# Ten buffers in turn for the pieces of x, four of them in the weights' space, each load issued behind a store

## The chip, the cores and the metric

The kernel runs on one core of a Trainium2 chip. The metric is the device time of one execution in microseconds (us). The times before are three executions of the same program; one more execution was taken by the hardware profiler, and all rows of "the profile" come from that one. Engine names are those of the profile: PE (TensorE, matrix products), DVE (VectorE), ACT (ScalarE), POOL (GpSimd), SP (SyncE, which here only issues transfers).

## The reference

One layer of a relational graph network on 12500 nodes with 256 features and 212500 edges, in float32. Its core, with eight relations (`edge_type` from 0 to 7) and edges sorted by `dst`:

```python
h  = maximum(layernorm(x), 0)
hx = einsum('ni,rio->rno', h, weight)            # 8 matrices of 256 x 256
agg = segment_sum(hx[edge_type, src], dst)       # sum over the edges of a node
out = x + agg * sqrt(0.5) + bias + (h @ loop_weight) * sqrt(0.5)
```

## The kernel before

**Order of the sums.** The kernel does not form `hx`. It first sums, for each node and each relation, the rows of h of its sources, and multiplies by the eight matrices afterwards. The edges are cut into 1581 tiles of up to 128. For each tile, 128 rows of 1 KB are fetched by their index into a message buffer (`msg`, `gather`, lines 922 to 946); this is an indirect transfer that POOL issues, one for each tile, save for 50 tiles whose rows SP and ACT fetch one by one. DVE makes a one-hot matrix for four tiles (`onehots`, L993), PE multiplies it with the message rows (`edge_sums`, L1031), and DVE adds the result of two tiles to an accumulator in a ring (`add_sums`, L1064). When a group of 128 nodes is complete, PE multiplies its accumulators with the eight matrices `w` and its own row of h with `wl` (`product`, L1238), and the result with x and the bias is stored.

**The start.** The rows of h, that is the normalised x, must be in memory before messages can be fetched from them. x is cut into 26 pieces (24 of 512 rows, 512 KB each; one of 128 rows; one of 84). A piece is loaded into a row buffer (`load_rows`, L886, on SP), DVE takes its statistics (`bn_stats`, L828), ACT takes the root (L864) and normalises it in place (L872, four instructions in a piece), and SP stores it to `h32` (`rest`, L895). `norm_rows(i)` does this for piece i; what it leaves for later runs in the `after` functions that `close` returns. Pieces 0 to 3 are done ahead of the main loop. In the loop over tiles t, three of four turns take one piece each, so that the last piece is taken at t = 28.

**Tiles from x.** The gathers begin before h32 exists. Tiles 0 to 99 are fetched from x itself, and their messages are normalised by DVE and ACT in the message buffer (`batch`, L1402, and `moments_by_scalar` for a share of the statistics on ACT). From tile 100 on gathers read h32 (`state["h32"]` = 28 + AHEAD, then LATE more); the first of them waits for all the stores.

**What sets the order.** All instructions are placed by hand (`tc.manual_schedule()`): each engine runs its instructions in the order in which this code issues them, and waits in that order. Four orders matter here.

- SP's queue carries the loads and stores of the pieces, the index loads (L390, L406, L418), then bias and weights (`load_weights`, L1363, issued at t = 28 behind the last store), then the rows of x and h of the node groups (`load_groups`, L1181). A load into a buffer waits on SP until the store of the buffer's last piece has landed. Before, `norm_rows(i)` first issues the load of piece i + 4, which takes the buffer of piece i - 2 among six; the store of piece i comes later, in `after`.
- POOL's gathers are issued ahead of the sums by `goal(t)` (L948): at most 24 + 2t early on, t + 65 later, with less lead from t = 170 on. Each gather also waits for the sums of the last pair of tiles issued before it (L945), and for its message buffer, one of 66 (33 pairs).
- ACT normalises pieces, then messages; at t = 34 it scales the weights (`scale_weights`, L1378), in place, in the order w (first half), wl, w (second half), wl.
- PE turns the rows of the first node group (L1088) soon after; these rows (`hr`) come from h32 by SP, behind the weights.

**The space of w.** `w` holds 128 partitions of 2 x 2048 floats, 16 KB in each partition, from the start of the kernel; a piece of x takes 4 KB in each partition. `rowp` has six row buffers (`ROWS`), which the pieces, the bias and later the rows of the node groups take in turn.

Of the kernel before, what the change touches and what calls it, by code (L numbers as in the profile page):

```python
# [9 lines left out]
F32 = mybir.dt.float32  # L10
# [13 lines left out]
P = 128  # L24
# [4 lines left out]
XG = 4  # L29
# [56 lines left out]
SHARED = 3  # L86

ROWS = 6
FIRST = 4


# [157 lines left out]
def kernel(  # L249
# [12 lines left out]
    N, D = x.shape  # L262
# [30 lines left out]
    w = const.tile([P, KC, R * D], F32, name="w")  # L293
# [34 lines left out]
    with ExitStack() as main:  # L328
# [4 lines left out]
        ep = main.enter_context(tc.tile_pool(name="ep", bufs=1))  # L333
        rowp = main.enter_context(tc.tile_pool(name="rowp", bufs=ROWS))
        idx = main.enter_context(tc.tile_pool(name="idx", bufs=2))
# [469 lines left out]
        for d in range(0, N, XG * P):  # L805
            k = min(XG, (N - d) // P)
# [4 lines left out]
        def rows_of(a, i):  # L811
            d, k, n = pieces[i]
            return a[d : d + k * n].rearrange("(k p) d -> p k d", p=n)
# [3 lines left out]
        def moments(rows_, n, then, begun=None):  # L817

            if not bunch:
                bunch.append(small.tile([P, 2 * BATCH, 6], F32, name="stats") if begun is None else begun)  # L820
                if n < P:
                    nc.vector.memset(bunch[0], 0.0)
            stats = bunch[0]
            here = rows_ if begun is None else rows_[:-SHARED]
            for row in rows_:
                k = sum(len(r) for r, _, _ in bunch[1:])
                if begun is None or len(bunch) - 1 < len(here):
                    in_run("stats", nc.vector.bn_stats(stats[:n, k, :], row), row is here[-1])  # L828
                bunch.append(([row], n, None))
            bunch.append(([], n, then))  # L830
# [49 lines left out]
        xts = {}  # L880

        def load_rows(i):
            if i < len(pieces):
                _, k, n = pieces[i]
                xts[i] = rowp.tile([P, XG, D], F32, tag="rows", name="xt")
                nc.sync.dma_start(xts[i][:n, :k, :], rows_of(x, i))  # L886

        def norm_rows(i):
            d, k, n = pieces[i]
            xt = xts.pop(i)  # L890
            if i > 1:
                load_rows(i + ROWS - 2)

            def rest():
                nc.sync.dma_start(rows_of(h32, i), xt[:n, :k, :])  # L895

            moments([xt[:n, j, :] for j in range(k)], n, rest)

# [103 lines left out]
        def load_offsets(u0):  # L1002
            n = min(REGS, NU - u0)
            b, q = row_of(u0)
            _, vals = nc.values_load_multi_w_load_instructions(
                place[b][0:1, q : q + n], engines=[DVE], min_val=0, max_val=RING - 1,
                skip_runtime_bounds_check_because="clamped to the ring where it is computed")
            for i, v in enumerate(vals):
                offsets[u0 + i] = v
# [279 lines left out]
        with tc.manual_schedule():  # L1289

            load = prepare(0)
            load[0]()
            for i in range(ROWS):
                load_rows(i)
            make_identity(nc, ident)
            iota_i = marks.tile([P, XG * GROUP], I32, tag="mark0", name="iota_i")
# [29 lines left out]
            for i in range(2):  # L1326
                norm_rows(i)
# [19 lines left out]
            after.pop(0)()  # L1347
            for i in range(2, FIRST):
                norm_rows(i)
# [83 lines left out]
            load_offsets(0)  # L1433
            done["norm"] = FIRST
            for t in range(0, 2 * BATCH, BATCH):
# [5 lines left out]
            for t in range(NT):  # L1441
# [12 lines left out]
                if t % BATCH == BATCH - 1:  # L1454
                    if done["norm"] < len(pieces):
                        after = batch(t + 1 + BATCH)
                    elif done["scaled"] <= t + 1 + 2 * BATCH:
                        after = batch(done["scaled"], 2 * BATCH)
                        after.append(lambda t=done["scaled"]: begin_batch(t))
                elif done["norm"] < len(pieces):  # L1460
                    for i in range(1 if NT > 400 else 20):
                        if done["norm"] < len(pieces):
                            norm_rows(done["norm"])
                            done["norm"] += 1
                            if t % BATCH % 2 or NT <= 400 or done["norm"] == len(pieces):
                                after += close()
                    if NT <= 400:
                        for f in after:
                            f()
                        after = []  # L1470
                    if done["norm"] == len(pieces):
                        for f in after:
                            f()
                        after = []
                        norms_end(t)
# [91 lines left out]
```

## Time and profile before

| what | value |
|---|---|
| median of three executions | 1952.6 us |
| lowest and highest | 1951.16 and 1956.97 us |
| the profiled execution | 1951.46 us |
| its span, first to last instruction | 1949.8 us |
| granted TensorE clock in it, mean | 0.953 of full speed |
| bytes moved by DMA in it | 279.41 MB |

How to read the rows. A row of a timeline gives start and length in us, engine, line, operation, output and inputs, how many instructions are merged in it (x8), and in brackets the idle time of the engine before it with what ended that idle time. A row of waits gives the engine and line that waited, what for, the total in us, how often, and the longest. A row of stretches gives the limits in us, the length, for each engine its busy time with the number of instructions (PE, PEld for weight loads, DVE, ACT, POOL), the granted clock, the mean busy share of the 16 DMA engines, and GB/s; a share over 1 arises where transfers overlap. Busy time does not hold waiting or the time to issue a transfer.

### The profile page before, as it was taken

How to read it: one execution, taken by the hardware profiler on the slowest of the kernel's cores; microseconds unless marked ns; L12 is line 12 of the kernel's file. 1: busy time of each engine (PE TensorE's matmuls, PEld its weight loads, DVE VectorE, ACT ScalarE, POOL GpSimd, SP SyncE). 2: the span in 40 equal slices, each digit the busy share in tenths (PEclk: the TensorE clock that was granted, in tenths of full speed). 3: DMA queues.
4: the chain of work that ended last, by engine and by line, in shares of the span. 5: the costliest groups of instructions: out<-in, count | busy, mean ns of one | idle time of the engine just before them, and what ended most of it. 6: DMA issues, size and time to landing. Idle time of an engine off the chain costs nothing.

```text
span 1949.8 us, 40539 instructions
## 1 busy us (share of the span) xinstructions
PE 1702.0 (87%) x10161; PEld 1460.0 (75%) x10161; DVE 1305.0 (67%) x3284; ACT 157.2 (8%) x333; POOL 1455.6 (75%) x1557
## 2 busy tenths in 40 slices
PE   2358999999998999889898899998889889899998
PEld 2247898998887777777777777777777777687887
DVE  7668766787765687656677665578566567665652
ACT  6778200000000000000000000000000000000000
POOL 7767777777777777777777777777777777777774
PEclk9559999999999999999999999999999999999999
DMA  9984454544444444444544444444444444444442
GB/s 291 329 281 129 125 152 123 153 133 141 122 142 131 132 143 114 138 131 121 152 132 121 141 128 124 142 121 142 131 120 140 130 125 132 121 141 126 131 121 82
DMA packets 158423, 279.41 MB, mean 143 GB/s; under 512 B 35441, under 2 KB 109191, under 8 KB 158183
## 3 DMA queue, kind: packets, MB, share of 16 engines
q0 software_dynamic: 73488, 200.77, 35.6%
q1 hardware_dynamic: 76648, 72.73, 12.1%
q10 hardware_dynamic: 8046, 3.30, 0.9%
q8 instruction: 80, 1.31, 0.3%
q14 instruction: 161, 1.31, 0.2%
HBM read 251.06 MB, written 25.60 MB: 142 GB/s over the span
## 4 chain that ended last, share of the span: by engine, by line
PE 40%; DMA 23%; POOL 20%; issue 8%; DVE 6%; ACT 3%; SPq 0%; DVEq 0%; POOLq 0%; ACTq 0%; PEldq 0%
PE po L1238 20%; DMA msg<-h,gidx 20%; POOL msg L936 20%; PE ps L1031 18%; ACT msg L872 1%; DVE acc L1064 1%; DMA h<-xt 1%; DVE stats L828 1%; DMA xt<-in_x_dram 1%; DVE acc L1106 1%; PE pt L1088 1%; ACT xt L872 1%; DMA msg<-h 1%; DVE oh L993 1%; PE pt L1137 1%
## 5 line engine op out<-in xcount | busy, mean ns | idle before, releaser
L936 POOL DMA_INDIRECT msg<-h,gidx x1431 | 1358.7, 949 | 437.4 <-issue 363.8
L1031 PEld LDWEIGHTS ps<-oh,msg 128*128 128x128 f32 x6324 | 929.1, 197 | 390.5 <-DMA msg<-h,gidx 248.4
L1031 PE MATMUL ps<-oh,msg 128*128 128x136 f32 (+1 forms) x6324 | 1010.5, 289 | 204.5 <-DMA msg<-h,gidx 120.8
L1238 PE MATMUL po<-w,acc 128*128 128x256 f32 (+1 forms) x3136 | 890.3, 389 | 7.8 <-DVE acc L1064 7.2
L1064 DVE TENSOR_TENSOR acc<-acc,ps 128x352 f32 x791 | 408.6, 517 | 391.2 <-PE ps L1031 381.9
L1238 PEld LDWEIGHTS po<-w,acc 128*128 128x128 f32 (+1 forms) x3136 | 519.4, 193 | 45.5 <-DVE acc L1064 10.4
L1106 DVE SCALAR_TENSOR_TENSOR acc<-types,pt 128x256 f32<-128x256 bf16 x688 | 248.6, 412 | 68.6 <-PE pt L1088 64.4
L993 DVE TENSOR_TENSOR oh<-fixed,cols 128x544 f32<-128x544 f32 x396 | 282.8, 714 | 0.0
L936 POOL DMA_INDIRECT msg<-in_x_dram,gidx x100 | 94.9, 949 | 39.2 <-issue 34.2
L1238 PE MATMUL po<-wl,self_t 128*128 128x256 f32 (+1 forms) x392 | 114.6, 418 | 6.8 <-DVE acc L1064 4.5
L1238 PEld LDWEIGHTS po<-wl,self_t 128*128 128x128 f32 (+1 forms) x392 | 72.9, 208 | 15.5 <-DVE acc L1064 5.6
L1226 DVE TENSOR_TENSOR xr<-xr,po 128x256 f32<-128x256 f32 (+1 forms) x98 | 40.5, 413 | 24.0 <-PE po L1238 17.3
L872 ACT ACTIVATE msg<-msg,shift,rstd 128x256 f32<-128x256 f32 x100 | 50.8, 587 | 6.3 <-DVE stats L836 4.6
L872 ACT ACTIVATE xt<-xt,shift,rstd 128x256 f32<-128x256 f32 x98 | 50.0, 587 | 13.1 <-DVE shift L869 13.1
L1253 DVE TENSOR_TENSOR xr<-xr,po 128x256 f32<-128x256 f32 (+1 forms) x98 | 41.2, 421 | 10.6 <-PE po L1238 7.3
L828 DVE BATCH_NORM_STATS2 stats<-xt 128x6 f32<-128x256 f32 x98 | 34.1, 411 | 14.9 <-DMA xt<-in_x_dram 14.6
L1088 PE MATMUL pt<-ident,hr 128*128 128x128 f32 (+1 forms) x196 | 39.0, 282 | 4.6 <-DMA hr<-h 2.7
L1093 DVE COPY self_t<-pt 128x256 f32<-128x256 f32 (+1 forms) x98 | 40.5, 414 | 3.1 <-PE pt L1088 2.9
L1160 DVE CAST types<-pt 128x512 bf16<-128x512 f32 x22 | 15.2, 691 | 40.5 <-PE pt L1156 40.5
L455 DVE TENSOR_SCALAR moves<-fixed 128x271 int32<-128x271 int32 (+1 forms) x90 | 40.5, 450 | 1.6 <-DVE acc L1064 0.5
L457 DVE COPY_PREDICATED fixed<-moves,fixed 128x311 int32<-128x311 int32 (+14 forms) x90 | 38.0, 422 | 3.1
L1088 PEld LDWEIGHTS pt<-ident,hr 128*128 128x128 f32 (+1 forms) x196 | 25.7, 152 | 7.1 <-DMA hr<-h 2.9
(166 smaller groups left out, 348.8 us busy)
## 6 DMA issues: line engine op xcount, KB each, us to landing
msg<-h ACTq DMA_DIRECT2D x3200, 1.0 KB
msg<-h SPq DMA_DIRECT2D x3200, 1.0 KB
msg<-h,gidx POOLq DMA_INDIRECT x1431, 4.7
xt<-in_x_dram SPq DMA_DIRECT2D x24, 512.0 KB
h<-xt SPq DMA_DIRECT2D x24, 512.0 KB
xr<-in_x_dram SPq DMA_DIRECT2D x23, 512.0 KB
hr<-h SPq DMA_DIRECT2D x23, 512.0 KB
out_dram<-xr SPq DMA_DIRECT2D x22, 512.0 KB
```

The lines of the kernel that those rows point to most:

```text
L455: nc.vector.tensor_single_scalar(m, packed[:, :n], 1 << (bit + k), op=ALU.bitwise_and)
L828: in_run("stats", nc.vector.bn_stats(stats[:n, k, :], row), row is here[-1])
L872: nc.scalar.activation(row, row, AF.Relu, bias=shift[:n, j : j + 1], scale=rstd[:n, j : j + 1])
L936: i = nc.gpsimd.indirect_dma_start(out=msg[t], out_offset=None, in_=table[:, :], in_offset=bass.IndirectOffsetOnAxis(ap=gidx[b][:, at : at ...
L993: j = nc.vector.tensor_tensor(o[:, k : k + v, :i, :width], iota_f[:, :width].unsqueeze(1).unsqueeze(1).to_broadcast([P, v, i, width]), of. ...
L1031: j = nc.tensor.matmul(ps[:, c, first : first + width], m[:, c * P : (c + 1) * P], o[:, :width], start=(i == 0 and c == 0), stop=(end and ...
L1064: i = nc.vector.tensor_tensor(a, a, ps, op=ALU.add)
L1088: in_run("turns", nc.tensor.transpose(pst[:, c, :n], rows_[:n, c * P : (c + 1) * P], ident[:n, :n]), c == KC - 1)
L1093: nc.vector.tensor_copy(got["self", g][:, :, :n], pst[:, :, :n])
L1106: i = nc.vector.scalar_tensor_tensor(acc[:, :, r, s0 : s0 + n], of, float(r + 1), pst[:, :, :n], op0=ALU.is_equal, op1=ALU.mult)
L1238: i = nc.tensor.matmul(got["out", g][:n], lhs, rhs, start=(r == R and c == 0), stop=(r == R - 1 and c == KC - 1))
L1253: nc.vector.tensor_add(rows_[:n, k, :], rows_[:n, k, :], got["out", g][:n])
```

## The change

The number of places for pieces of x goes from six to ten (`STAGED`). Piece i takes place i mod 10; places 0 to 5 are row buffers as before, places 6 to 9 are quarters of the space of `w`, which the weights fill later. Ten loads are issued at the start instead of six. From then on the load of piece i + 8 is issued right behind the store of piece i, in `rest`, where before the load of piece i + 4 was issued at the start of `norm_rows(i)`, ahead of that store. Both wait for the store of piece i - 2, whose place they take. The pieces that take the quarters of `w` are 6 to 9 and 16 to 19. Of 26 pieces, 18 take a row buffer, three for each of the six, so the tiles that follow in `rowp` begin at the first buffer.

```diff
 ROWS = 6
+STAGED = 10
 FIRST = 4
...
         def load_rows(i):
             if i < len(pieces):
                 _, k, n = pieces[i]
-                xts[i] = rowp.tile([P, XG, D], F32, tag="rows", name="xt")
+                j = i % STAGED - ROWS
+                if j < 0:
+                    xts[i] = rowp.tile([P, XG, D], F32, tag="rows", name="xt")
+                else:
+                    xts[i] = w.rearrange("p c (a k d) -> p (c a) k d", k=XG, d=D)[:, j, :, :]
                 nc.sync.dma_start(xts[i][:n, :k, :], rows_of(x, i))
 
         def norm_rows(i):
             d, k, n = pieces[i]
             xt = xts.pop(i)
-            if i > 1:
-                load_rows(i + ROWS - 2)
-
             def rest():
                 nc.sync.dma_start(rows_of(h32, i), xt[:n, :k, :])
+                if i > 1:
+                    load_rows(i + STAGED - 2)
 
             moments([xt[:n, j, :] for j in range(k)], n, rest)
...
             load = prepare(0)
             load[0]()
-            for i in range(ROWS):
+            for i in range(STAGED):
                 load_rows(i)
             make_identity(nc, ident)
```

## The prediction, made before the result was known

> **What bounds the kernel now.** I read the page first, then the gathers on POOL as a timeline, then stretches of the span.
>
> ```profile
> span 1949.8 us, 40539 instructions
> PE 1702.0 (87%) x10161; PEld 1460.0 (75%) x10161; DVE 1305.0 (67%) x3284; ACT 157.2 (8%) x333; POOL 1455.6 (75%) x1557
> ```
>
> PE looks like the bound at 87%, POOL like a bystander at 75%. But POOL's share leaves out the issue gap of about 0.30 us after each gather. The stretch from 205.7 us to the last gather counts them:
>
> ```profile
> 205.70:1933.00 1727.30, 1588.52 (x9610) 1361.73 (x9609) 1149.80 (x2746) 6.92 (x4) 1307.21 (x1377) 0.98 0.46 132
> ```
>
> 1377 gathers in 1727.3 us are 1.254 us each, which is 0.949 busy plus 0.305 of gap: POOL runs without a stop from 205.7 us on, and the other engines follow its data. The timeline of POOL (start, length, idle before in brackets) holds every stop:
>
> ```profile
> 4.86 1.11 POOL L936 DMA_INDIRECT msg<-in_x_dram,gidx  x1 [2.23 <-DVE bound_o L1320]
> ...
> 94.01 0.95 POOL L936 DMA_INDIRECT msg<-in_x_dram,gidx  x1 [0.30 <-issue]
> 100.54 0.94 POOL L936 DMA_INDIRECT msg<-in_x_dram,gidx  x1 [5.59 <-issue]
> ...
> 109.29 0.95 POOL L936 DMA_INDIRECT msg<-in_x_dram,gidx  x1 [0.30 <-issue]
> 112.07 0.94 POOL L936 DMA_INDIRECT msg<-in_x_dram,gidx  x1 [1.83 <-issue]
> ...
> 137.06 0.95 POOL L936 DMA_INDIRECT msg<-h,gidx  x1 [0.30 <-ACT wl L1379]
> ...
> 203.69 0.95 POOL L936 DMA_INDIRECT msg<-h,gidx  x1 [0.30 <-issue]
> 205.66 0.95 POOL L936 DMA_INDIRECT msg<-h,gidx  x1 [1.01 <-ACT msg L872]
> ...
> 1931.94 0.95 POOL L936 DMA_INDIRECT msg<-h,gidx  x1 [0.30 <-issue]
> ```
>
> Three stops beyond 0.30 us: 5.29, 1.53 and 0.71, together **7.53 us**. Removing them is all that an earlier start phase can give; what follows is POOL's own pace and a fixed tail of 17.9 us (1949.8 less 1931.94).
>
> What are they waits for? Counting POOL's rows, the gather at 100.54 is that of tile 72, emitted in turn 26 and tied by L945 to the sums of tile 25; that at 112.07 is tile 80, tied to tile 29; that at 205.66 is tile 154, tied to tile 89, whose message buffer it reuses. PE's timeline answers to it (tile 25 ends early in the first row, tile 29 in the second, tile 89 is the last row):
>
> ```profile
> 99.02 2.09 PE L1031 MATMUL ps<-oh,msg 128*128 128x104 f32 x8 [5.72 <-DVE acc L1064]
> 110.55 2.09 PE L1031 MATMUL ps<-oh,msg 128*128 128x104 f32 x8 [2.13 <-DVE acc L1064]
> 137.98 0.54 PE L1088 MATMUL pt<-ident,hr 84*128 84x84 f32 x2 [2.70 <-DMA hr<-h]
> 203.89 0.99 PE L1031 MATMUL ps<-oh,msg 128*128 128x104 f32 x4
> ```
>
> So two gates: the pieces being normalised up to turn 29, and the tiles normalised on ACT and DVE (28 to 99) up to tile 89. **First gate.** The waits of SP and DVE, then ACT's timeline:
>
> ```profile
> SPq L886 <- DMA h<-xt: 57.6, 18, 6.4
> DVE stats L828 <- DMA xt<-in_x_dram: 14.6, 6, 3.1
> ```
>
> ```profile
> 69.95 0.30 ACT L864 ACTIVATE rstd<-spread,eps 128x8 f32<-128x8 f32 x1 [1.57 <-DVE spread L862]
> 83.45 0.30 ACT L864 ACTIVATE rstd<-spread,eps 128x8 f32<-128x8 f32 x1 [3.85 <-DVE spread L862]
> 98.58 0.30 ACT L864 ACTIVATE rstd<-spread,eps 128x8 f32<-128x8 f32 x1 [5.52 <-DVE spread L862]
> 110.11 0.30 ACT L864 ACTIVATE rstd<-spread,eps 128x8 f32<-128x8 f32 x1 [1.93 <-DVE spread L862]
> 131.43 1.91 ACT L1378 ACTIVATE w<-w 128x2048 f32<-128x2048 f32 x1
> 134.79 1.91 ACT L1378 ACTIVATE w<-w 128x2048 f32<-128x2048 f32 x1 [1.15 <-DMA w<-in_L_gnn_weight_dram]
> ```
>
> SP stands 57.6 us in 18 waits for a store before it may refill the buffer. The late pieces then cost DVE 14.6 us, and ACT's four idle times sum to 12.87 us (10.94 by turn 25). **Second gate.** The second half of w lands only at 134.8 us, and ACT, in order, normalises no tile past it meanwhile; hr, behind w on SP, stops PE at 137.98.
>
> **The change part by part.** The transfers that it moves, from the list of DMA issues:
>
> ```profile
> xt<-in_x_dram SPq DMA_DIRECT2D x24, 512.0 KB
> h<-xt SPq DMA_DIRECT2D x24, 512.0 KB
> w<-in_L_gnn_weight_dram SPq DMA_DIRECT2D x2, 1024.0 KB
> ```
>
> *The loads.* These 24 loads and stores, and two small ones each, are issued as before, all on SP, 12.8 MB in and 12.8 MB out; only order and distance move. Nothing is added to DVE, ACT, PE or POOL. Ten loads go out first instead of six; the four more stand behind those that pieces 0 to 5 need, and ahead of stores 0 and 1, for which only load 10 waits. Load i+4 (asked for ahead of store i) becomes load i+8 (behind it). It still waits for store i-2, but is needed eight pieces later, not four.
>
> *The wait on SP.* Behind a waiting load stand store i+1, later the loads of block 1 (needed from turn 44), then the weights. While SP waits, store i-1, load i+7 and store i are still out, some 1.5 MB; before, the wait for the last store emptied SP's work. The gaps show in the stretches (last columns: clock, DMA share, GB/s):
>
> ```profile
> 0.00:134.80 134.80, 45.53 (x172) 39.06 (x173) 93.38 (x352) 93.81 (x185) 95.22 (x125) 0.66 0.96 310
> 4.00:20.00 16.00, 0.95 (x4) 0.44 (x3) 14.52 (x68) 4.53 (x10) 11.72 (x12) 1.00 1.05 341
> 32.00:36.00 4.00, 4.00 (x20) 4.00 (x20) 3.10 (x12) 4.00 (x6) 3.09 (x4) 1.00 0.60 152
> 64.00:80.00 16.00, 6.92 (x24) 5.65 (x24) 10.50 (x37) 12.72 (x26) 12.29 (x13) 0.50 1.05 354
> 100.00:104.00 4.00, 1.30 (x7) 1.04 (x6) 3.86 (x14) 3.67 (x8) 2.84 (x3) 0.50 0.64 217
> 104.00:112.00 8.00, 3.68 (x14) 3.17 (x15) 5.47 (x19) 5.46 (x12) 4.73 (x5) 0.50 1.07 372
> 124.00:136.00 12.00, 6.39 (x26) 5.62 (x25) 4.54 (x15) 10.67 (x24) 8.96 (x11) 0.50 1.07 340
> ```
>
> The mean to 134.8 us is 310 GB/s; stretches without a gap hold 341, 354, 372 and 340, weighted 350. In the full stretch from 64 us POOL still issued 13 gathers in 16 us, so full DMA does not slow POOL.
>
> *Gate one* needs turn 25 to be 100.54 - 95.26 = 5.3 us earlier and turn 29 6.8 us. If the loads are there, ACT's idle gives 10.9 and 12.9. Both stops go.
>
> *Gate two* depends on bytes. By 134.8 us 41.8 MB had moved (310 x 134.8), 0.4 of them before 4 us. With POOL 7.5 us ahead, the gathers issued by 127.3 us are those of 134.8 before, so the same 41.8 MB must be through for w to land 7.5 us earlier: 41.4 MB in 123.3 us, 336 GB/s. At 350 w lands at 4 + 118.3 = 122.3, 12.5 us earlier; at 310 nothing moves. I take 350, since the deeper order is meant to remove just these gaps and the row nearest to it (64 to 80) shows 354. Normalisation ends some 10 us earlier, so ACT reaches w at about 120 and waits a little there: w is what is late next, but no longer on POOL's path. Tile 89 then moves by more than 7.5 us and POOL's own pace binds.
>
> *The space of w.* Its last pieces are 16 to 19, stored long before the weights are asked for behind store 25: nothing. If that cover failed, w would only land later, the price of gate two.
>
> *h32.* POOL's first gather from h (137.06) needs all stores, and would come at 137.06 - 6.82 = 130.2. Needed by then: 12.8 MB of loads, as much of stores, 0.9 of indices (six tiles of 131 to 160 KB) and 100 gathers of 128 rows of 1 KB, 13.1 MB; together 39.6 MB; at 350 this is through at 116. Nothing.
>
> **Sum:** -7.53 us. The profiled execution took 1951.46, 1.1 below the median of 1952.6; it comes to 1943.9, and from the median to **1945.1**.
>
> **Rivals.** *A: the engines are simply full.* DMA share is 0.96 to 134.8 us. Were 1.00 the ceiling, w could land at 134.8 x 0.96 = 129.4, 5.4 us earlier, and the time is 1947.2; with less of the gaps filled, anything up to 1951.5. For it: the same bytes. Against it: 1.05 to 1.07 over 8 to 16 us at a time. The Trainium skill ("DMA: Bandwidth & Descriptors", Issuing engines are not separate DMA queues) says that transfers of all issuing engines run on the same 16 DMA engines and interleave. By that rule loads asked for earlier only take their share from gathers and stores, which is this rival; the trace agrees that the share is near full, and the gaps of 0.60 and 0.64 speak for what is left.
>
> *B: no change.* The rate stays at 310, or the pieces in w are waited for as one buffer, so that the loads come no earlier: gate two stays, 1952.6. Against it: the 57.6 us of SP waits go with the distance.
>
> *C: slower.* Stores stand behind loads that wait, so h32 is complete late and POOL stops at its first gather from h. Each us past 130.2 costs one; at 137.7 the gain is gone. That needs 39.2 MB to take 133.7 us, 293 GB/s or less; at 270 the stores end at 149.2, and the time is 1952.6 + 149.2 - 137.7 = 1964.1. For it: SP is in order, and its longest wait is 6.4 us. Against it: no long stretch is under 310.
>
> **How the numbers follow.** Forecast 0.56; A 0.20; B 0.11; C 0.13. The forecast lies within 1943.0 (1 us under the profiled sum) and 1946.7; A within 1946.7 and 1951.5; B about 1952.6. The range 1943.0 to 1953.0 leaves out C and a part of B. 0.3% is 5.9 us, about what a measurement of this kernel can tell from no change. Faster by more is the forecast, 0.56; within it A and B, 0.31; slower C, 0.13.
>
> **What would show it.** POOL without idle over 0.35 us between 90 and 210; no DVE wait for xt, or one under 3 us; SP's wait for stores no longer in front of late pieces; w scaled by 125; DMA at 340 GB/s or more from 4 to 115 us. Wrong, if POOL stops at its first gather from h (C), if it stops again near tile 154 with w at 128 or later (A), or if DVE still waits for xt by 10 us or more (B).

## The result and the profile after

The changed kernel takes 1942.36 us (median of six, 1941.88 to 1944.0); the kernel before, beside it, 1952.89 us (1951.08 to 1956.97). The ratio is 0.995, 95% interval 0.994 to 0.996: 10.5 us or 0.54% faster, where 7.5 us were forecast. The median lies 0.6 us under the low end of the stated range. Eight of the twelve experiments fell on two chips on which the kernel before takes some 2405 us; they are compared only with it on the same chip.

The page of the changed kernel:

```profile
span 1942.2 us, 40543 instructions
PE 1696.5 (87%) x10161; PEld 1457.2 (75%) x10161; DVE 1304.4 (67%) x3284; ACT 156.7 (8%) x333; POOL 1456.5 (75%) x1557
```

The shares are those of before; from them alone nobody would see what changed. POOL as a stretch, then as a timeline:

```profile
210.00:1920.00 1710.00, 1563.43 (x9457) 1339.75 (x9456) 1132.41 (x2688) 3.82 (x2) 1294.19 (x1363) 0.98 0.45 132
```

```profile
130.02 0.95 POOL L940 DMA_INDIRECT msg<-h,gidx  x1 [0.30 <-ACT unused L839]
...
197.86 0.95 POOL L940 DMA_INDIRECT msg<-h,gidx  x1 [0.30 <-issue]
...
1925.12 0.95 POOL L940 DMA_INDIRECT msg<-h,gidx  x1 [0.31 <-issue]
```

The pace is 1.255 us for a gather (1710 by 1363), as before. All three stops are gone: no idle of POOL between the second gather and the last is over 0.32 us. The first gather from h comes at 130.02, without a wait (130.2 was forecast), and the gather of tile 154, which stopped before, at 197.86.

The waits of SP and DVE to 140 us, then ACT's timeline at the weights:

```profile
SPq L891 <- DMA h<-xt: 14.5, 8, 3.9
SPq L891 <- DMA h<-w: 2.0, 3, 1.1
DVE stats L829 <- DMA xt<-in_x_dram: 0.4, 1, 0.4
```

```profile
117.97 1.91 ACT L1382 ACTIVATE w<-w 128x2048 f32<-128x2048 f32 x1
121.27 1.91 ACT L1382 ACTIVATE w<-w 128x2048 f32<-128x2048 f32 x1 [1.09 <-DMA w<-in_L_gnn_weight_dram]
```

SP's waits for a store, ahead of a load, fell from 57.6 to 16.5 us. DVE waits for xt once, for 0.4 us, where it waited 14.6 us in six places. ACT runs without the four idle times: from the root at 68.18 to that at 77.67 it takes 9.49 us for three pieces, where the same turn took 13.50 us before (69.95 to 83.45). The second scaling of w (that of its second half, which lands last) starts at 121.27 instead of 134.79. The DMA from 20 to 100 us, the kernel before first, then the changed one, and for the latter also the stretch from 4 to 115 us that the prediction names:

```profile
20.00:100.00 80.00, 27.69 (x107) 24.28 (x107) 55.39 (x198) 62.64 (x117) 56.75 (x60) 0.65 0.97 316
```

```profile
20.00:100.00 80.00, 30.23 (x127) 27.03 (x126) 65.43 (x235) 72.72 (x139) 60.48 (x65) 0.70 1.03 363
4.00:115.00 111.00, 39.73 (x161) 34.88 (x161) 90.82 (x342) 87.00 (x170) 83.48 (x88) 0.72 1.01 348
```

From 20 to 100 us the share rose from 0.97 to 1.03 only, the rate from 316 to 363 GB/s. The signs that the prediction set for its forecast are there: no stop, DVE's wait under 3 us, w scaled by 125, and 348 GB/s from 4 to 115 us where 340 or more was asked.

### The profile page after: what moved, and what is told of

The parts are those of the page before. It is cut to its first block, busy times and chain, and to the rows that moved or that the text cites. A ratio compares the mean times of both kernels' runs of the same rounds, so it can differ in the third digit from the quotient of the medians.

```text
span 1942.2 us, 40543 instructions
## 1 busy us (share of the span) xinstructions
PE 1696.5 (87%) x10161; PEld 1457.2 (75%) x10161; DVE 1304.4 (67%) x3284; ACT 156.7 (8%) x333; POOL 1456.5 (75%) x1557
## 4 chain that ended last, share of the span: by engine, by line
PE 38%; POOL 22%; DMA 21%; issue 9%; DVE 6%; ACT 3%; SPq 0%; DVEq 0%; POOLq 0%; ACTq 0%
POOL msg L940 22%; PE po L1242 19%; DMA msg<-h,gidx 19%; PE ps L1035 17%; ACT msg L873 1%; DVE acc L1068 1%; DVE stats L829 1%; DMA w<-in_L_gnn_weight_dram 1%; DMA xt<-in_x_dram 1%; PE pt L1092 1%; DVE oh L997 1%; DVE moves L456 0%; DMA h<-xt 0%; ACT acc L1081 0%; ACT xt L873 0%
## 5 line engine op out<-in xcount | busy, mean ns | idle before, releaser
L940 POOL DMA_INDIRECT msg<-in_x_dram,gidx x100 | 94.8, 948 | 32.2 <-issue 23.8
L873 ACT ACTIVATE xt<-xt,shift,rstd 128x256 f32<-128x256 f32 x66 | 33.7, 588 | 10.3 <-DVE shift L870 10.3
L829 DVE BATCH_NORM_STATS2 stats<-msg 128x6 f32<-128x256 f32 x79 | 27.3, 410 | 0.6 <-issue 0.6
```

What stands on the lines that cost most here:

```text
L873: nc.scalar.activation(row, row, AF.Relu, bias=shift[:n, j : j + 1], scale=rstd[:n, j : j + 1])
L940: i = nc.gpsimd.indirect_dma_start(out=msg[t], out_offset=None, in_=table[:, :], in_offset=bass.IndirectOffsetOnAxis(ap=gidx[b][:, at : at ...
```

## The experiments

Three readings compete. **P**: what counts is the sum of POOL's stops (its idle times beyond the usual 0.30 us), and these are set by the two gates of the start phase that the prediction describes. **D**: the time follows the moment at which the weights land (read from the start of the second scaling of w), one for one. **O**: the place of the load behind the store does it, not the number of buffers. Kernels with "again" in the label are the same code on another chip.

### Distance alone: ten places, the load ahead of the store

```diff
         xt = xts.pop(i)
+        if i > 1:
+            load_rows(i + STAGED - 2)
         def rest():
             nc.sync.dma_start(rows_of(h32, i), xt[:n, :k, :])
-            if i > 1:
-                load_rows(i + STAGED - 2)
```

> Ten places, but the load of piece i + 8 is issued at the start of norm_rows(i), ahead of the store of piece i, as before; only the distance is changed, not the place behind the store. Theory P (the time falls by POOL's three stops, 7.5 us, and those go with the distance): DVE has no wait for xt over 1 us, POOL no idle over 0.35 us between 90 and 210 us, and the time is within 1.5 us of the changed kernel (1941 to 1944). Rival O (the place behind the store does it): stores again stand behind waiting loads, and at least half of the gain is lost, 1947 to 1953. Rival D (the time follows the moment at which the weights land, 121.3 us in the changed kernel): the time changes by as much as the start of the second scaling of w does.

> The same as e1_ahead (ten places, the load of piece i + 8 ahead of the store of piece i), wanted on a chip where the kernel before takes about 1953 us. Theory P: no wait of DVE for xt, no stop of POOL over 0.35 us between 90 and 210 us, 1941 to 1944 us. Rival O: 1947 to 1953. Rival D: as much off 1942.4 as the second scaling of w is off 121.3. If the kernel before takes 2400 us again, within 0.3%.

The first run took 2408.01 us, ratio 1.0007 (0.9982 to 1.0033), on a chip of 2405 us. On a chip of 1953.7 us it took **1949.3**, ratio 0.998 (0.9969 to 0.999): 4.4 us faster, well under half of the change's 10.5. P's number (1941 to 1944) was wrong; O's for this run (1947 to 1953) holds; D, with the second scaling 10.48 us later than in the changed kernel, gives 1952.8. POOL and ACT of this run show what was left:

```profile
141.51 0.95 POOL L941 DMA_INDIRECT msg<-h,gidx  x1 [1.72 <-ACT unused L842]
144.12 0.94 POOL L941 DMA_INDIRECT msg<-h,gidx  x1 [0.42 <-issue]
148.64 0.96 POOL L941 DMA_INDIRECT msg<-h,gidx  x1 [1.07 <-issue]
202.48 0.94 POOL L941 DMA_INDIRECT msg<-h,gidx  x1 [2.80 <-ACT msg L873]
...
1929.16 0.94 POOL L941 DMA_INDIRECT msg<-h,gidx  x1 [0.30 <-issue]
```

```profile
126.49 1.91 ACT L1383 ACTIVATE w<-w 128x2048 f32<-128x2048 f32 x1 [4.95 <-DMA w<-in_L_gnn_weight_dram]
131.75 1.91 ACT L1383 ACTIVATE w<-w 128x2048 f32<-128x2048 f32 x1 [3.04 <-DMA w<-in_L_gnn_weight_dram]
```

```profile
SPq L891 <- DMA h<-xt: 38.6, 10, 8.0
SPq L891 <- DMA h<-w: 15.8, 4, 5.5
```

```profile
20.00:100.00 80.00, 30.10 (x119) 26.61 (x119) 62.55 (x226) 70.06 (x132) 60.53 (x64) 0.65 0.99 323
```

The first gate is open: POOL has no stop before 141 us, though DVE still waits 4.7 us for xt in three places, where P expected no wait over 1 us. The second is not: ACT waits 8 us for w. SP again stands 54.4 us in front of loads, and for ACT in front of a store it waits only 10.4 us (43.0 in the changed kernel): the stores behind the loads are mostly ready. DMA runs at 323 GB/s, and the weights come behind late stores. POOL's stops are 4.81 us, all of them behind the first scaling of w.

### Order alone: six places, the load behind the store

```diff
-STAGED = 10
+STAGED = 6
```

> Six places only, none in the space of w, but the load (of piece i + 4) is issued behind the store of piece i: the order alone. Theory P: the load is asked for later than before with the same four pieces of lead, so DVE's waits for xt are at least the 14.6 us of before, POOL's stops at tiles 72 and 80 stay or grow by up to 10 us, and the time is 1950 to 1962. Rival O: 1942 to 1947. Rival D: as the second scaling of w moves against 134.8 us, one for one.

> The same as e2_six_behind (six places, the load of piece i + 4 behind the store of piece i), wanted on a chip where the kernel before takes about 1953 us. In the first job every kernel took some 2405 us, POOL stopped for 2 to 8 us again and again through the whole span, and nothing done in the start phase could be seen in the time. Theory P: DVE waits for xt in nine places for some 15 us as there, POOL's stops at tiles 72 and 80 stay, 1950 to 1962 us. Rival O (the order does it): 1942 to 1947. If the kernel before takes 2400 us again, all are within 0.3%.

The first took 2409.34 us, ratio 1.0004 (0.9979 to 1.0028). The second, on the chip of 1953.7 us, took **1952.57**, ratio 0.9989 (0.998 to 0.9999). O, by which this would have taken 1942 to 1947, falls; P's 1950 to 1962 holds. D, with w scaled 1.08 us earlier than before, can't be told from P here. POOL's larger stops:

```profile
85.93 0.94 POOL L940 DMA_INDIRECT msg<-in_x_dram,gidx  x1 [1.02 <-PE ps L1035]
92.03 0.94 POOL L940 DMA_INDIRECT msg<-in_x_dram,gidx  x1 [1.40 <-issue]
98.57 0.94 POOL L940 DMA_INDIRECT msg<-in_x_dram,gidx  x1 [1.85 <-issue]
104.28 0.94 POOL L940 DMA_INDIRECT msg<-in_x_dram,gidx  x1 [1.01 <-issue]
110.69 0.95 POOL L940 DMA_INDIRECT msg<-in_x_dram,gidx  x1 [1.72 <-issue]
204.14 0.94 POOL L940 DMA_INDIRECT msg<-h,gidx  x1 [0.58 <-ACT msg L873]
...
1930.74 0.95 POOL L940 DMA_INDIRECT msg<-h,gidx  x1 [0.30 <-issue]
```

```profile
DVE stats L829 <- DMA xt<-in_x_dram: 16.7, 10, 2.7
```

```profile
133.71 1.91 ACT L1382 ACTIVATE w<-w 128x2048 f32<-128x2048 f32 x1 [1.44 <-DMA w<-in_L_gnn_weight_dram]
```

```profile
20.00:100.00 80.00, 28.28 (x111) 24.27 (x110) 56.70 (x200) 64.72 (x121) 57.90 (x62) 0.62 0.98 327
```

The first gate is back as six small stops, one of 0.09 us not shown, with DVE waiting 16.7 us for xt, and the second half of w is scaled at 133.71: 5.87 us of stops, 5.59 of them by 111 us. SP now waits for no store ahead of a load; it stands 70.7 us in front of stores whose pieces ACT has not normalised (21.6 us before), and the loads behind them are issued late. So neither part alone fills the gaps (327 and 323 GB/s); only both do (363).

### The price of the second gate: a copy ahead of the weights

```diff
             def norms_end(t):
                 state["h32"] = t + AHEAD
+                copy = dram.tile([4096, D], F32, name="copy")
+                for k in range(0, 4096, 512):
+                    nc.sync.dma_start(copy[k : k + 512], x[k : k + 512])
                 load_weights()
```

> The changed kernel with a copy of 4096 rows of x within memory (8 x 512 KB, SP, not needed by anything) issued right ahead of the weights, so that w and hr land later, some 12 to 18 us. Theory P with the second gate as predicted: w may be scaled up to 127.3 us without cost; beyond it each us costs one in POOL's stops near tile 154. With the second scaling at 133 to 139 POOL stops for 6 to 12 us in all and the median is 1948 to 1955. Rival S (the tiles from x have slack of their own, w does not count): no stop, 1941 to 1944. Rival D: the full delay, 1954 to 1961.

> The same as e4_w_late (the changed kernel, with a copy of 4 MB within memory on SP right ahead of the weights), wanted on a chip where the kernel before takes about 1953 us; the last job fell on one where it takes 2407 and every engine stops for some us again and again. Theory P: the second scaling of w at 133 to 139 us, POOL's stops 6 to 12 us in all, most of them near tile 154, the last gather at 1924.4 us plus their sum within 1 us, median 1948 to 1955 us. Rival S (w does not count): no stop, 1941 to 1944. Rival D (the full delay of w): 1954 to 1961.

The first took 2410.85 us, ratio 1.0025 (0.9996 to 1.0053), beside 2407.09. The second took **1954.08** beside 1954.44, ratio 0.9999 (0.9989 to 1.0008): with the copy nothing is left of what the change brought, though the pieces come as early as in the changed kernel (DVE waits 0.2 us for xt).

```profile
119.24 0.94 POOL L940 DMA_INDIRECT msg<-in_x_dram,gidx  x1 [0.42 <-DMA msg<-in_x_dram,gidx]
123.81 0.94 POOL L940 DMA_INDIRECT msg<-in_x_dram,gidx  x1 [3.62 <-DMA msg<-in_x_dram,gidx]
125.67 0.95 POOL L940 DMA_INDIRECT msg<-in_x_dram,gidx  x1 [0.91 <-DMA msg<-in_x_dram,gidx]
145.53 0.94 POOL L940 DMA_INDIRECT msg<-h,gidx  x1 [1.42 <-ACT unused L842]
148.14 1.18 POOL L940 DMA_INDIRECT msg<-h,gidx  x1 [0.41 <-issue]
152.65 0.96 POOL L940 DMA_INDIRECT msg<-h,gidx  x1 [0.71 <-issue]
175.05 0.94 POOL L940 DMA_INDIRECT msg<-h,gidx  x1 [1.44 <-ACT msg L873]
206.71 0.95 POOL L940 DMA_INDIRECT msg<-h,gidx  x1 [1.88 <-ACT msg L873]
...
1933.19 0.95 POOL L940 DMA_INDIRECT msg<-h,gidx  x1 [0.30 <-issue]
```

```profile
136.22 1.91 ACT L1382 ACTIVATE w<-w 128x2048 f32<-128x2048 f32 x1 [2.44 <-DMA w<-in_L_gnn_weight_dram]
```

The second scaling came 14.95 us later than in the changed kernel (136.22 against 121.27). The profiled executions differ by 8.4 us (1952.38 and 1944.0), as POOL's stops do (8.41). That fits P's rule, by which the first 6 us of delay are free and the other 8.9 are paid; S (no cost) falls, and by the profile D (14.95) too. The medians differ by 11.7, between P and D; they come from two chips.

The delay of w is not the only thing that the copy does. 4.05 of the 8.41 us fall at 119 to 126, ahead of both scalings, in front of gathers from x while the copy runs; the gathers issued from 104 to 118 us took a median of 10.7 us to land, where it was 6.2 in the changed kernel. What holds POOL there isn't settled. By P's rule a stop taken early is one that w no longer causes, as in the kernel before, but only the 4.36 us from 145 us on lie behind w here, and of these 1.58 at tile 154, where the expectation had most of the 6 to 12 us. The cleaner price of a late w is that of distance alone: 4.81 us, all behind w, where the rule gives 4.5.

### Where three more microseconds could come from

> The changed kernel once more, for a second profile and a second comparison. Its median was 10.5 us under that of before, while POOL's stops in the profiles differ by 7.5 us. If the 3 us between are scatter of the runs, the difference of the medians here lies between 6.5 and 9.5 us; if the change brings more than the stops, it is again 10 us or more, and the last gather starts as much earlier than at 1931.9 us.

> The changed kernel once more, beside the one before on the same chip. Theory P: POOL without a stop over 0.35 us from the first gather on, last gather at 1924.4 to 1925.4 us, median 1941 to 1944 us, times within 3 us of each other. If the chip is one on which the kernel before takes 2400 us, no difference.

> The kernel before once more, for a second profile. Theory P: its last gather starts at 1924.4 us (1931.94 less the 7.5 us of stops in its first profile) plus the sum of POOL's stops in this profile, within 1 us, whatever that sum is; and if the 3 us between the medians' difference (10.5) and the difference of the profiles (7.5) come from stops that differ between executions, its times scatter over 5 to 8 us and the changed kernel's over 2 to 3. Rival: the scatter lies elsewhere, the last gather is off that sum by more than 2 us.

> The kernel before once more, for a second profile of it and many times, on a chip where it takes about 1953 us. Theory P: its last gather starts at 1924.4 us plus the sum of POOL's stops in this profile, within 1 us, and that sum differs from the 7.5 us of the first profile by as much as the time of the profiled execution differs from 1951.5. If the 3 us by which the medians fell further than the profiles come from stops that differ between executions, this sum is between 5 and 13 us and the times scatter over 5 us or more, where the changed kernel's six lie within 2.2. Rival: the same stops and yet another time, so that the scatter lies behind the last gather or in the pace of POOL.

Three of these four fell on the chips of 2405 us: the changed kernel 2404.32, ratio 0.9987 (0.9967 to 1.0007), and 2404.23, ratio 0.9987 (0.9964 to 1.0009); the kernel before 2410.49 beside itself, ratio 1.0 (0.9973 to 1.0027). The change can't be seen there, and a second comparison of the changed kernel on a chip of the usual time is missing. A wait of POOL and a stretch of the kernel before on such a chip:

```profile
POOL msg L936 <- PE ps L1031: 288.0, 185, 6.6
```

```profile
205.00:2300.00 2095.00, 1662.16 (x9242) 1454.54 (x9241) 1127.38 (x2723) 21.89 (x39) 1269.54 (x1338) 0.89 0.37 106
```

POOL needs 1.566 us for a gather here (2095 by 1338) and waits for PE 185 times. That a few microseconds won at the start are lost again in the next of these waits is likely, but not shown. Why these chips stop so often, the trace doesn't tell.

The last, the kernel before on another chip of its usual time, took 1952.69 (profiled execution 1952.69, times 1951.36 to 1955.16), ratio to itself 0.9999 (0.999 to 1.0008):

```profile
99.46 0.94 POOL L936 DMA_INDIRECT msg<-in_x_dram,gidx  x1 [4.54 <-issue]
104.75 0.94 POOL L936 DMA_INDIRECT msg<-in_x_dram,gidx  x1 [0.61 <-issue]
112.58 0.94 POOL L936 DMA_INDIRECT msg<-in_x_dram,gidx  x1 [3.15 <-issue]
154.22 0.95 POOL L936 DMA_INDIRECT msg<-h,gidx  x1 [0.68 <-issue]
207.83 0.95 POOL L936 DMA_INDIRECT msg<-h,gidx  x1 [2.64 <-PE ps L1031]
210.60 0.94 POOL L936 DMA_INDIRECT msg<-h,gidx  x1 [0.58 <-issue]
...
1932.78 0.94 POOL L936 DMA_INDIRECT msg<-h,gidx  x1 [0.30 <-issue]
```

```profile
136.55 1.91 ACT L1378 ACTIVATE w<-w 128x2048 f32<-128x2048 f32 x1 [2.40 <-DMA w<-in_L_gnn_weight_dram]
```

Its stops sum to 10.40 us, not 7.53, so the same program does not stop alike in two executions. The rest of the expectation fails. The last gather should come at 1924.4 plus the stops and is 2.0 us earlier: without the stops it would be at 1922.38, so POOL's pace scatters too, by some 1.3 ns in a gather. The stops grew by 2.9 us and the profiled execution by 1.2. And the eleven times lie within 3.8 us, where 5 or more were expected.

### Half of the added places, and fewer gathers

> Eight places, two of them in the space of w: six pieces of lead instead of eight. Theory P: the gain stops as soon as POOL has no stop left. Turn 25 has to be 5.3 us and turn 29 6.8 us earlier than before, w 7.5 us; two more pieces of lead hide some 6 us of landing each, so most or all of it is there: 1942 to 1946, and the weights may be scaled later than in the changed kernel (121.3) without any cost as long as it is before 127. Rival D: half the places, half the gain, about 1947.5, and a later w costs one for one.

> The changed kernel with every 24th tile instead of every 28th fetched row by row by SP and ACT (59 tiles instead of 50), so that POOL issues 9 gathers less. Theory P (POOL's pace of 1.254 us for each gather sets the end): 9 x 1.254 = 11.3 us less, 1929 to 1933 us. Rival: PE, 87% busy, or SP and ACT, which have 1152 more row transfers to issue, take over the bound: 1938 to 1950 us.

`STAGED = 8` took 2404.49, ratio 1.0002 (0.9977 to 1.0027); it fell on a chip of 2405 us and tells nothing between P and D. `SINGLE = 24` instead of 28, so that every 24th tile is fetched row by row, took 2564.6, ratio 1.0664 (1.0623 to 1.0704). It is 157 us slower on a chip of 2407 us, where SP's row transfers (L965) already hold 32.2% of the chain that ended last in the kernel before; with `SINGLE = 24` they hold 40.7% (L969). On a chip of the usual time it was not run; whether nine gathers less bring 11 us there stays open.

## Why the prediction was right, and where it was not

All profiled executions on chips of the usual time, with POOL's stops over 0.30 us summed from the rows shown, and the gate's rule from the prediction (w may start its second scaling at 127.3 for nothing, and each us beyond costs one). "Behind it" is the time from the second scaling to the gather of tile 154.

| kernel | second scaling of w | less 127.3 | POOL's stops | tile 154, behind it | last gather less stops | median |
|---|---|---|---|---|---|---|
| before | 134.79 | 7.5 | 7.53 | 70.87 | 1924.41 | 1952.89 |
| before, second profile | 136.55 | 9.3 | 10.40 | 71.28 | 1922.38 | 1952.69 |
| order alone | 133.71 | 6.4 | 5.87 | 70.43 | 1924.87 | 1952.57 |
| distance alone | 131.75 | 4.5 | 4.81 | 70.73 | 1924.35 | 1949.3 |
| both (the change) | 121.27 | under 0 | 0 | 76.59 (no stop) | 1925.12 | 1942.36 |
| both, w late | 136.22 | 8.9 | 8.41 | 70.49 | 1924.78 | 1954.08 |

- **The bound.** Right. POOL's unbroken pace sets the end, and what a kernel can win at the start is the sum of its stops. The last gather less the stops is the same within 0.8 us in five of six rows, whatever was changed.
- **Gate one.** Right: the gathers tied to turns 25 and 29 came in time with distance, also with the load ahead of the store.
- **Gate two.** Right in price and, with one addition, in place. The first row agrees with the rule by construction (127.3 is 134.8 less the 7.5 us of its stops); in the four other rows with stops the sum is within 1.2 us of the rule, though gate one or the copy took a part of it first (6.82 of 7.53 before, 5.59 of 5.87 with order alone). The gate can be read more directly: wherever the gather of tile 154 was held, it left 70.4 to 71.3 us behind the second scaling. In the changed kernel it came unheld at 197.86, which less 70.4 to 71.3 gives 126.6 to 127.4 as the latest start without cost. The addition: with distance alone 2.31 of the 4.81 us were taken at 141 to 149 us already, by the gathers of tiles 108, 110 and 113, which the prediction did not foresee.
- **w or hr.** Both come late together, and no run moved hr alone. But PE's first use of hr lies 2.9 to 3.6 us behind the second scaling, and the gather of tile 154 does not follow these differences (it is earliest, at 70.43, where hr is at 3.45, and latest, at 71.28, where hr is at 3.27), while the last batch of ACT before that gather starts 64.4 to 64.6 us behind the scaling in all six. That speaks for w, through ACT, as the prediction has it.
- **When w lands.** Its second scaling lay at 121.27, where 122.3 was worked out from 350 GB/s; the rate from 4 to 115 us was 348. This gate decides: opening only the first one (distance alone) leaves the loss to be taken at the second.
- **What opens gate two.** The prediction named distance as the cause and treated the place behind the store as a part of it. That was too little: with distance alone SP still stood 54.4 us ahead of loads, and the second half of w was scaled at 131.75. Both are needed, as the rates show.
- **The size.** This is the term that was mis-sized: 7.53 us of stops were read from one profiled execution, and the medians differ by 10.5. The two profiled executions differ by 7.46 (1951.46 and 1944.0), which is closer to 7.53 than the parts deserve: the last gather came 6.82 us earlier, and the tail behind it, called fixed in the prediction, shrank from 17.9 to 17.1 (17.1 to 18.2 in the six profiles). A second profile of the kernel before has 10.40 us of stops; its times reach from 1951 to 1957, and those of the changed kernel, which has nothing left to stop for, from 1941.9 to 1944.0, with the profiled one the slowest. That stops differ between executions is shown; how the 3 us divide between them, POOL's pace and the tail is not.
- **Rivals.** A (DMA full at a share of 1.00) fell: the share was 1.03 from 20 to 100 us, and the rate rose by 15%. The Trainium skill ("DMA: Bandwidth & Descriptors", Issuing engines are not separate DMA queues) says that transfers of all issuing engines run on the same 16 DMA engines and interleave. The late landing of gathers beside the copy (10.7 us against 6.2) agrees with that; A failed because gaps were left, which the new order filled. B and C did not come; h32 was ready at 130.02, when POOL asked for it.

## What to carry to other kernels

Where an engine of modest busy share works without a stop to the end, list its idle times above its usual gap: their sum is all that an earlier start can win, and the last gate that it meets decides how much of it is won. In this kernel a prefetch in an in-order queue needed both distance and place: a load that waits should stand behind the store that is ready, and far enough ahead of its use. Either alone left the rate at 323 to 327 GB/s, where both gave 363. Sum stops over several executions before taking them as a size.

## What the runs showed of the hardware

- The mean busy share of the DMA engines said little here about what was left: 0.97 moved 316 GB/s and 1.03 moved 363, 0.98 moved 327 and 0.99 moved 323, all over the same 80 us and with the same kinds of transfers.
- Two of the chips ran the same program in some 2405 us instead of 1953, with granted clocks of 0.87 to 0.89 instead of 0.95 to 0.96 and stops of some us in POOL all along the span (some 465 us beyond the usual gap in one profile, 7.5 on a usual chip); an effect of 0.5% is not visible there.
- While a copy of 4 MB within memory ran, POOL's gathers stopped for 4.05 us in all and took 10.7 us to land instead of 6.2, in the one profile that has it; by what they were held is open.
